# Attention scores of four heads on sixteen 32x32 tiles of TensorE instead of four strips of 32x128

## The chip, the cores and the metric

The kernel runs on one core of a Trainium2 chip. The metric is the device time of one execution in microseconds (us); the median of three runs is given, and beside it one execution that the hardware profiler recorded. TensorE (PE in the profile, its weight loads PEld) multiplies, VectorE (DVE) and ScalarE (ACT) work elementwise, GpSimd is POOL, SyncE is SP. SBUF is the working memory, and PSUM the memory that TensorE writes its results to.

## The reference, cut to what matters

Four layers are added to an image x of shape (2, 128, 64, 64) one after the other, each on a group-normalized x. Layer 1 is made of convolutions, layer 2 of a Fourier transform with products in the frequency domain, layer 3 is an attention with eight heads. The change is in layer 0, whose first attention has 4 heads of 32 channels over 64 x 64 = 4096 tokens:

```python
q1, k1, v, q2, k2 = jnp.split(qkv, 5, axis=1)
...
attn1 = jax.nn.softmax(jnp.einsum('bhnc,bhmc->bhnm', q1, k1) * temperature, axis=-1)
out1 = jnp.einsum('bhnm,bhmc->bhnc', attn1, v)
attn2 = jax.nn.softmax(jnp.einsum('bhnc,bhnd->bhcd', q2, k2) * temperature, axis=-1)
out2 = jnp.einsum('bhnc,bhcd->bhnd', v, attn2)
out = out1 + out2
```

Queries and keys are normalized beforehand. All of it is float32.

## The kernel before, in words

`tile_conv_preact_kernel` keeps x in SBUF and runs the four layers one after the other. A second, general version follows behind a flag and isn't executed with this input.

In layer 0 (`_layer0`, L1155) the 128 channels are the partitions: head j has partitions 32j to 32j+31 of `q1` and `k1`, each 128 x 4096. For each of the two batches the kernel first makes queries, keys and the first values, and then runs the attention `_attn_four` (L1084). That function goes over 8 blocks of 512 queries (`qb`) and, inside, 32 tiles of 128 keys (`kt`), 512 iterations over both batches. One iteration does the following.

- It takes two tiles `ps_s` of PSUM, each with two banks of 512 float32 per partition: the first for heads 0 and 1, the second for heads 2 and 3. The pool behind them, `spp`, has three such tiles (`bufs=3`), so the second tile of an iteration is the one that held the first pair's scores an iteration earlier. It can be written when the exponential of that pair has read it.
- Four matmuls (L1092), one for each head j, write the scores. The stationary operand is 32 channels x 128 keys of `k1`, the moving operand 32 channels x 512 queries of `q1`. Rows 32j to 32j+31 of the array are used with all 128 columns: a strip. The result is 128 keys x 512 queries, on all partitions of one bank; each head has its own bank.
- Two exponentials on ACT (L1102), each over one `ps_s` tile (128 x 1024), write the `weights` tiles in SBUF. `f0_p`, their pool, has six of them.
- `multiply` of the iteration *before* is called (a list `waiting` keeps it back by one). In it `four` (L1440) has four matmuls with a stationary operand of 128 keys x 32 channels of `vt` and a moving operand of 128 keys x 512 queries of the weights: all rows of the array, 32 columns for each head. They add into the accumulator `accs[0]`.
- For the softmax's sums, DVE adds the weights of four iterations (`sums`, L1459 and L1461, two instructions in each of three iterations out of four), and once in four iterations `four` multiplies the result with ones into `accs[1]`.

After 32 key tiles the accumulator is divided by the sums (L1469 to L1473).

A float32 matmul is two passes in TensorE's program, first and second pass side by side, each a weight load (LDWEIGHTS) and a MATMUL. So the four score matmuls are 8 loads and 8 MATMUL records in the profile, and so are the four value matmuls.

The order of work on each engine is the order in which the code issues it. The waits between engines are made by the tile framework from the tiles that are read and written: the first score matmul into a `ps_s` tile carries the wait for that tile, and the exponential waits for the last matmul of its pair. After every iteration `_layer0` (L1521) lets a generator `side` go one step further, two in the first 32 iterations: the remaining `values`, the channel attention of the second branch, and the normalization of the next batch. These steps put matmuls, transposes, DVE and ACT work between the iterations, until they are used up; then iterations follow on one another with nothing between them. `_attn_four` is called in layer 0 alone; layer 3 has an attention of its own (L1679, L1698).

Of the kernel before, what the change touches and what calls it, by code (L numbers as in the profile page):

```python
# [18 lines left out]
CH = 512  # L19
# [1064 lines left out]
def _attn_four(nc, p_pool, ps_pool, q, k, multiply):  # L1084

    waiting = []
    for qb in range(NCH):
        for kt in range(NQT):
            ps = [ps_pool.tile([128, 2, CH], F32, tag="sp", name="ps_s") for _ in range(2)]
            for j in range(4):  # L1090
                rows = slice(32 * j, 32 * j + 32)
                nc.tensor.matmul(  # L1092
                    ps[j // 2][:, j % 2, :],
                    k[rows, kt * 128 : (kt + 1) * 128],
                    q[rows, qb * CH : (qb + 1) * CH],
                    start=True,
                    stop=True,
                )
            w = []
            for p in range(2):  # L1100
                w.append(p_pool.tile([128, 2, CH], F32, tag="weights", name="weights"))
                nc.scalar.activation(w[p], ps[p], AF.Exp)  # L1102
            waiting.append((qb, kt, w))
            if len(waiting) > 1:
                multiply(*waiting.pop(0))
            yield
    for x in waiting:
        multiply(*x)
    yield
# [45 lines left out]
def _layer0(ctx, tc, X, a, cst, eps5, worst):  # L1155
# [354 lines left out]
    for b in range(B):  # L1510
        ss = small.tile([128, 4, 2 * len(BLOCKS)], F32, tag="ss", name="ss")
        w2 = small.tile([128, 128], F32, tag="w2", name="w2", bufs=1)
        ready[0] = 0
        run(queries_keys(ss))
        scale_queries(ss)
        run(values((0, 1)))
        side = [values((2, 3, 4)), channel_attention(ss, w2)]
        if b + 1 < B:
            side.append(normalize(b + 1))
        side = chain(*side)  # L1520
        for n, _ in enumerate(_attn_four(nc, pp, spp, q1, k1, multiply)):  # L1521
            next(side, None)
            if n < 32:
                next(side, None)
        run(side)
        run(finish(b, w2))
# [345 lines left out]
```

## Time and profile before

| what | value |
|---|---|
| median of 3 runs | 4988.65 us (4988.64 to 4990.94) |
| the profiled execution | 4991.73 us |
| its span, first to last instruction | 4989.9 us |
| mean granted clock of TensorE | 0.914 of full speed |
| busy: PE / ACT / DVE | 4458.1 / 3153.4 / 2291.3 us |
| instructions: PE, and as many weight loads | 38084 |
| score matmuls L1092, first and last start | 173.6 and 1933.1 us |
| layer 3's attention, first and last start of L1679 | 2995.7 and 4970.4 us |

A line of the costliest groups reads: line, engine, operation, output<-inputs, partitions x elements, count, then busy time and mean duration in ns of one, then the idle time of the engine just before and what ended most of it. Busy time is the union of overlapping instructions: eight matmuls that run side by side for 1 us are 1 us. For TensorE the form "32\*128" names the rows and columns of the array that are used. The chain that ended last is followed back from the last instruction to whatever released it; its shares add up to the span. In the 40 slices each digit is a busy share in tenths, and a slice is 125 us.

### The profile page before, as it was taken

What the parts mean: (1) busy time and instruction counts of PE and PEld (TensorE: products, weight loads), DVE (VectorE), ACT (ScalarE), POOL (GpSimd) and SP (SyncE); (2) the same over time, 40 slices, a digit from 0 to 9 for tenths busy, and PEclk for the clock granted to TensorE, in tenths of its full rate; (3) what the DMA queues carried; (4) which work ended last, traced back from release to release, by engine and by line L of the source; (5) the groups of instructions that cost most, each with busy time, mean ns of one, the idle gap of its engine ahead of it and who ended that gap; (6) DMA issues with size and microseconds to landing.
All of it is one profiled execution on the core that took longest, in us unless ns stands there. A gap on an engine that the chain in (4) does not pass through costs nothing.

```text
span 4989.9 us, 87747 instructions
## 1 busy us (share of the span) xinstructions
PE 4458.1 (89%) x38084; PEld 1792.5 (36%) x38084; DVE 2291.3 (46%) x3050; ACT 3153.4 (63%) x3539; POOL 53.4 (1%) x102
## 2 busy tenths in 40 slices
PE   6678899996889997996676789999999999999998
PEld 3222222241222223445565673333333333333332
DVE  5777678767777877997111142310122013100010
ACT  2445468824556884201011118999999999999998
POOL 1000000000000001000000000000000000000000
PEclk9788899997889999998676659999999999999999
DMA  1000000000000000006887600000000000000000
GB/s 40 0 1 1 1 1 1 1 1 1 1 1 1 1 1 6 1 0 108 126 127 121 89 7 3 5 5 6 5 5 5 6 5 5 5 6 5 6 5 6
DMA packets 154494, 90.06 MB, mean 18 GB/s; under 512 B 24553, under 2 KB 148457, under 8 KB 154098
## 3 DMA queue, kind: packets, MB, share of 16 engines
q1 hardware_dynamic: 154098, 84.36, 10.4%
q8 instruction: 300, 4.92, 0.4%
q14 instruction: 96, 0.79, 0.1%
HBM read 75.94 MB, written 4.19 MB: 16 GB/s over the span
## 4 chain that ended last, share of the span: by engine, by line
PE 78%; DVE 14%; issue 5%; ACT 2%; POOL 1%; DMA 0%; SPq 0%; ACTq 0%; DVEq 0%; POOLq 0%
PE ps_acc L1698 21%; PE ps_s L1679 17%; PE ps_acc L1440 11%; PE ps_s L1092 10%; DVE qk L1253 3%; PE ps_freq L827 3%; PE ps_acc L1315 2%; DVE X L612 2%; DVE sums L1461 2%; PE ps_pe L794 2%; DVE v L1253 2%; PE ps_bank L771 1%; PE ps_po L946 1%; PE ps_sp L1227 1%; DVE sums L1459 1%
## 5 line engine op out<-in xcount | busy, mean ns | idle before, releaser
L1689 ACT ACTIVATE weights<-ps_s 128x1024 f32<-128x1024 f32 x2048 | 1887.0, 1098 | 82.6 <-PE ps_s L1679 76.5
L1102 ACT ACTIVATE weights<-ps_s 128x1024 f32<-128x1024 f32 x1024 | 994.1, 1021 | 332.8 <-PE ps_s L1092 319.9
L1698 PE MATMUL ps_acc<-weights,vt 128*32 128x512 f32 x8192 | 1095.2, 607 | 0.0
L1679 PE MATMUL ps_s<-q,k 32*128 32x512 f32 x8192 | 926.6, 445 | 4.1 <-ACT weights L1689 3.3
L1092 PE MATMUL ps_s<-q,k 32*128 32x512 f32 x4096 | 686.6, 668 | 100.8 <-ACT weights L1102 100.7
L1679 PEld LDWEIGHTS ps_s<-q,k 32*128 32x128 f32 x8192 | 471.1, 183 | 847.5 <-ACT weights L1689 764.6
L1461 DVE TENSOR_TENSOR sums<-sums,weights 128x1024 f32<-128x1024 f32 x512 | 604.2, 1219 | 90.8 <-ACT weights L1102 90.8
L1440 PE MATMUL ps_acc<-weights,vt 128*32 128x512 f32 x4096 | 593.4, 633 | 12.0 <-ACT weights L1102 8.0
L1720 DVE COPY u<-ps_acc 128x512 f32<-128x512 f32 x32 | 22.1, 691 | 1005.3 <-PE ps_acc L1698 1005.3
L1092 PEld LDWEIGHTS ps_s<-q,k 32*128 32x128 f32 x4096 | 214.3, 191 | 535.9 <-issue 286.5
L1459 DVE TENSOR_TENSOR sums<-weights 128x1024 f32<-128x1024 f32 x256 | 303.7, 1218 | 192.3 <-ACT weights L1102 192.3
L1698 PEld LDWEIGHTS ps_acc<-weights,vt 128*32 128x32 f32 x8192 | 163.8, 108 | 379.1 <-issue 366.8
L612 DVE SCALAR_TENSOR_TENSOR X<-g,w,X 128x512 f32<-128x512 f32 x400 | 266.8, 741 | 0.1
L1440 PEld LDWEIGHTS ps_acc<-weights,vt 128*32 128x32 f32 x4096 | 85.6, 110 | 431.3 <-issue 393.4
L827 PE MATMUL ps_freq<-e,w_i 128*32 128x16 f32 x4224 | 140.2, 221 | 76.3 <-issue 76.3
L827 PE MATMUL ps_freq<-e,w_r 128*32 128x16 f32 x4224 | 142.8, 221 | 64.9 <-issue 64.4
L1253 DVE SCALAR_TENSOR_TENSOR qk<-pad,wd,qk 128x896 f32<-128x896 f32 (+2 forms) x160 | 171.1, 1069 | 4.1
L1440 PE MATMUL ps_acc<-sums,ones 128*32 128x512 f32 x1024 | 162.7, 608 | 3.5 <-DVE sums L1461 3.4
L827 PEld LDWEIGHTS ps_freq<-e,w_i 128*32 128x32 f32 x4224 | 131.9, 159 | 80.9 <-issue 80.8
L827 PEld LDWEIGHTS ps_freq<-e,w_r 128*32 128x32 f32 x4224 | 133.2, 159 | 69.1 <-issue 68.3
L837 ACT COPY pz<-ps_freq 128x272 f32<-128x272 f32 x16 | 6.8, 425 | 217.0 <-PE ps_freq L827 217.0
L837 DVE COPY pz<-ps_freq 128x256 f32<-128x256 f32 x16 | 6.8, 425 | 279.8 <-PE ps_freq L827 203.0
(237 smaller groups left out, 3276.7 us busy)
## 6 DMA issues: line engine op xcount, KB each, us to landing
w_r<-in_L_conv_kr_w SPq DMA_DIRECT2D x15, 528.0 KB, 12.2
w_r<-in_L_conv_kr_x SPq DMA_DIRECT2D x15, 528.0 KB
w_r<-in_L_conv_kr_y SPq DMA_DIRECT2D x15, 528.0 KB, 12.1
w_r<-in_L_conv_kr_z SPq DMA_DIRECT2D x15, 528.0 KB, 11.9
w_i<-in_L_conv_ki_w SPq DMA_DIRECT2D x15, 528.0 KB, 5.6
w_i<-in_L_conv_ki_x SPq DMA_DIRECT2D x15, 528.0 KB, 7.9
w_i<-in_L_conv_ki_y SPq DMA_DIRECT2D x15, 528.0 KB, 10.1
w_i<-in_L_conv_ki_z SPq DMA_DIRECT2D x15, 528.0 KB, 12.1
```

The source lines that it names most:

```text
L612: nc.vector.scalar_tensor_tensor(xi, g[:, i : i + ROWS, j : j + W], w8[:, s : s + 1], xi, ALU.mult, ALU.add)
L794: nc.tensor.matmul(pe[:, j * 6 * FW : j * 6 * FW + n * 3 * FW], yt[:, (r + j) * 128 : (r + j + 1) * 128], fwd_w[:, : n * 3 * FW], start=Tr ...
L827: nc.tensor.matmul(out.rearrange("p (x c) -> p x c", c=2), ws[n][:, :, s * FW + fw], e[:, s, :, :, 1 - n : 3 - n, fw].rearrange("p r b e - ...
L1092: nc.tensor.matmul(ps[j // 2][:, j % 2, :], k[rows, kt * 128 : (kt + 1) * 128], q[rows, qb * CH : (qb + 1) * CH], start=True, stop=True,)
L1102: nc.scalar.activation(w[p], ps[p], AF.Exp)
L1253: nc.vector.scalar_tensor_tensor(out, win, wd[:, grp, t : t + 1], out, ALU.mult, ALU.add)
L1440: nc.tensor.matmul(accs[n][rows, :], lhs(rows), w[j // 2][:, j % 2, :], start=first, stop=last)
L1459: nc.vector.tensor_add(parts[p], held[p], w[p])
L1461: nc.vector.tensor_add(parts[p], parts[p], w[p])
L1679: nc.tensor.matmul(ps[j // 2][:, j % 2, :], k[rows, kt * 128 : (kt + 1) * 128], q[n][rows, qb * CH : (qb + 1) * CH], start=(n == 0), stop= ...
L1689: nc.scalar.activation(w[p], ps[p], AF.Exp)
L1698: nc.tensor.matmul(ac[0][32 * j : 32 * j + 32, :], vt[:, kt, j // 2, i : i + 2, :].rearrange("p a d -> p (a d)"), w[j // 2][:, i, :], star ...
```

## The change

Each head's score matmul is cut into four by its keys. Strip i of 32 keys becomes a stationary operand of 32 channels x 32 keys, and its result goes to partitions 32i to 32i+31 of the same bank as before: a 32x32 tile of the array for each of four heads j and four strips i. The loop over strips is the outer one, so that all four heads come in turn within a strip. Sixteen matmuls with the same moving operands as before (each head's 512 queries are now streamed to four tiles) fill the same two `ps_s` tiles; exponentials, value matmuls and everything else stay as they are.

```diff
-            for j in range(4):
-                rows = slice(32 * j, 32 * j + 32)
-                nc.tensor.matmul(
-                    ps[j // 2][:, j % 2, :],
-                    k[rows, kt * 128 : (kt + 1) * 128],
-                    q[rows, qb * CH : (qb + 1) * CH],
-                    start=True,
-                    stop=True,
-                )
+            for i in range(4):
+                for j in range(4):
+                    rows, keys = slice(32 * j, 32 * j + 32), slice(32 * i, 32 * i + 32)
+                    nc.tensor.matmul(
+                        ps[j // 2][keys, j % 2, :],
+                        k[rows, kt * 128 + 32 * i : kt * 128 + 32 * i + 32],
+                        q[rows, qb * CH : (qb + 1) * CH],
+                        start=True,
+                        stop=True,
+                    )
```

## The prediction

> **What bounds the kernel now.** I read the page's slices first, then the chain that ended last, the costliest groups, the busy time of two stretches, the timeline of a few microseconds, and at last the starts of single instructions in it.
>
> ```profile
> PE   6678899996889997996676789999999999999998
> DVE  5777678767777877997111142310122013100010
> ACT  2445468824556884201011118999999999999998
> PEclk9788899997889999998676659999999999999999
> ...
> PE ps_acc L1698 21%; PE ps_s L1679 17%; PE ps_acc L1440 11%; PE ps_s L1092 10%; DVE qk L1253 3%; PE ps_freq L827 3%; PE ps_acc L1315 2%; DVE X L612 2%; DVE sums L1461 2%; PE ps_pe L794 2%; DVE v L1253 2%; PE ps_bank L771 1%; PE ps_po L946 1%; PE ps_sp L1227 1%; DVE sums L1459 1%
> ...
> L1102 ACT ACTIVATE weights<-ps_s 128x1024 f32<-128x1024 f32 x1024 | 994.1, 1021 | 332.8 <-PE ps_s L1092 319.9
> ...
> L1092 PE MATMUL ps_s<-q,k 32*128 32x512 f32 x4096 | 686.6, 668 | 100.8 <-ACT weights L1102 100.7
> ...
> L1440 PE MATMUL ps_acc<-weights,vt 128*32 128x512 f32 x4096 | 593.4, 633 | 12.0 <-ACT weights L1102 8.0
> ...
> L1092 PEld LDWEIGHTS ps_s<-q,k 32*128 32x128 f32 x4096 | 214.3, 191 | 535.9 <-issue 286.5
> ```
>
> One slice is 125 us. Layer 0's attention lies in 174 to 1938 us, and the changed matmuls (L1092) alone hold 10% of the chain. There are 2 batches x 8 query blocks x 32 key tiles = 512 iterations; 4096 records for 2048 score matmuls say that a float32 matmul is two passes, each with its own weight load.
>
> ```profile
> 800.00:900.00 100.00, 100.00 (x756) 26.19 (x752) 78.61 (x68) 80.62 (x84) 0.00 (x0) 1.00 0.00 1
> ...
> 400.00:500.00 100.00, 84.68 (x527) 25.07 (x530) 70.20 (x64) 58.69 (x64) 0.31 (x2) 0.87 0.00 1
> ```
>
> The columns after the length are PE, PEld, DVE, ACT, POOL, granted clock, DMA share and GB/s. In the first stretch there is no side work: TensorE never rests, at full clock. The same stretch holds 336 score records at eight an iteration, so 42 iterations in 100 us, **2.38 us each**. In the second, side work alternates with the attention and DVE shares the chain.
>
> ```profile
> 763.52 1.31 PE L1092 MATMUL ps_s<-q,k 32*128 32x512 f32 x8
> 764.76 1.94 ACT L1102 ACTIVATE weights<-ps_s 128x1024 f32<-128x1024 f32 x2 [0.18 <-PE ps_s L1092]
> 764.76 1.06 PE L1440 MATMUL ps_acc<-weights,vt 128*32 128x512 f32 x8
> 765.76 1.20 PE L1092 MATMUL ps_s<-q,k 32*128 32x512 f32 x8
> 766.89 1.06 PE L1440 MATMUL ps_acc<-weights,vt 128*32 128x512 f32 x8
> ```
>
> ```profile
> 779.93 1.00 PE ps_acc L1440 x8
> 780.92 1.07 PE ps_s L1092 x8
> 781.99 1.00 PE ps_acc L1440 x8
> 782.99 1.24 PE ps_s L1092 x8
> 784.23 1.54 PE ps_acc L1440 x8
> ```
>
> The second fence is the chain: the score group takes 1.07 and 1.24 us in turn, the value group 1.00. Every fourth iteration has a second group of ones, about 0.86 us more. The single starts show why 1.07 and 1.24 alternate. Three score tiles are in PSUM and an iteration takes two, so the second pair (heads 2, 3) waits for the exponential of the *first* pair of the iteration before. In a 1.24 group, heads 2 and 3 start some 180 ns after heads 0 and 1; in a 1.07 group, 13 ns or so after when that exponential is already done.
>
> **The numbers of one iteration**, from those starts at full clock:
> - weight load plus matmul of the next tile follow 6.7 ns after those of the tile before, though each matmul's second pass lies between them in program order: the second pass waits on its own tile and holds up no other.
> - first pass to second pass on one tile: 533 ns with 32x128 weights, 453 with 128x32 weights. Less 427 of streaming (512 columns; the value group's 8 records in two rounds show it), 106 and 26 remain: the first load, which nothing hides.
> - last second pass to the first instruction of the next group in another shape: 518 to 521 ns.
> - second pass of head 1 to the start of its exponential: 695 ns. Start of an exponential to the release of the score tile: 1075. Two exponentials start 920 apart.
>
> **What the Trainium skill says.** "TensorE: Matmul & The Clock Gate", section LDWEIGHTS, has a load take columns / 1.2 ns: 107 ns for 128 and 27 for 32; the 106 and 26 above agree. The same page, Part 3, gives 10.6x for sixteen 32x32 tiles with N=512, some 4 ns per tile, outputs in a bank for each row group: the arrangement of this change. No 32x32 matmul is in the trace of before; its 6.7 ns a tile in row and in column tiling is the nearest row. That part also says that matmuls keep program order; the trace differs, as second passes start after first passes of later tiles. "TensorEngine Tiling (Array Packing)", Key Properties, says that a change of mode drains the array; the 518 to 521 ns, some 92 over the streaming, agree, and both changes of mode remain.
>
> **The change part by part.**
> 1. *Passes on the array.* Four matmuls with 32x128 weights become sixteen with 32x32: 32 matmuls and 32 loads per iteration, for 8 and 8. If sixteen tiles run as independently as four rows or four columns do, each streams two passes as before. No gain or loss in streaming.
> 2. *Shorter first load*: 533 to 453, so 80 ns less per score group.
> 3. *Longer dispatch*: the last tile starts 15 x 6.7 = 100 ns after the first, for 20. Group length without a wait: 100 + 453 + 518 = 1.071, for 20 + 533 + 518 = 1.071. Points 2 and 3 cancel. The step's unknown size in 32x32 mode is bounded by about 1.7 ns (the offset between a load and its matmul here) and by 30 (four instructions at the 7.5 ns each that the layer 2 products at L827 sustain, 134 starts in 1 us). I take 6.7.
> 4. *The order of the wait.* The loop over key strips is outside that over heads. Head 2 of strip 0 is the third matmul of sixteen, and it is the one that waits for the score tile. Behind it on TensorE's queue stand thirteen others, among them strips 1 to 3 of heads 0 and 1. So the first pair is finished only after the wait; ACT's next exponential and then the value group wait for that. Before, heads 0 and 1 went ahead of it.
>
> The loop through this wait: third matmul to fourteenth (strip 3, head 1) 11 x 6.7 = 74; its second pass 453; exponential starts 695; release 1075: **2.297 us from one wait to the next**. TensorE alone needs 1.071 + 0.994 (value group) = 2.065. So each plain iteration that follows another waits 0.231 us. Before, the loop was 6 + 533 + 695 + 1075 = 2.309 from the *start* of the group, and a held second pair didn't delay the first, so the iteration after a held one had no wait: 2.296, 2.065, 3.156 (with ones), 2.065, sum 9.58 for four. (Measured: 4 x 2.38 = 9.52, so the recurrence is 0.6% long.) After: 2.300, 2.300, 3.160, 2.070, sum 9.83. The change makes three waits in four iterations of what were two: 0.25 / 4 = **0.062 us per iteration**.
>
> 5. *Where it counts.* The starts of the score groups give 286 iterations in the two plain stretches (700 to 1010 and 1560 to 1950 us), 225 in the others. Of these, DVE's side work ends many waits, and by the chain TensorE's attention lines, ACT's exponential and PE's other groups hold roughly 0.6 of the stretch; the rest hides it. 286 + 0.6 x 225 = 421 iterations x 0.062 = **26 us**. If nothing were hidden it is 32, if all of it in the mixed stretches 18.
> 6. *Added instructions* in PE's stream, 512 x 48 = 24,576 matmuls and loads: at zero, on the assumption that TensorE reads them in during the 1 us value group; without that cover, see the second rival. ACT, DVE, DMA and all other layers are untouched.
>
> The profiled execution has 4989.9 us of span and 1.8 around it, 4991.7 in all, 3 over the median of 4988.65. 4991.7 + 26 = 5017.8 for such a one, 4988.65 + 26 = **5015** for the median.
>
> **The rivals.**
> - *Not slower.* The shorter load wins: if the step per tile is below about 1.8 ns, as the 1.7 between load and matmul would allow, then the loop is 2.223 + 11 x 1.7 = 2.242 and the group 80 - 26 = some 50 ns shorter, and the recurrence falls to the 2.395 of before or just under. Price: down to -0.02 us x 421 = -9, so 4980 to 4990. For it: loads are a quarter as long. Against: 6.7 ns in both tilings. Chance 0.15 (0.05 of it below by over 0.2%).
> - *The sequencer can't keep up*: steps of 10 to 30 ns. Both the loop (11 steps) and the group (15) grow; 12 ns of average per ns of step, so at 20 ns 0.22 us x 421 = 92 us, 5080; at 30 ns 5130. For it: 64 instructions where 16 were, in bursts longer than any that the trace shows at 1.7 ns. Against: TensorE has a microsecond before each burst. Chance 0.17.
> - *Sixteen tiles aren't sixteen queues.* The trace never holds more than four second passes back at once. If only about eight can be, the tiles run in two waves, 0.45 us more in the loop and the group: 0.5 x 460 = 230 us, 5220. If tiles of one row group take turns, 3 x 0.88 us more for every iteration: 2.7 x 512, about 6370. For it: no such row in the trace. Against: one tile's second pass stops neither other rows in row tiling nor other columns in column tiling, which one queue per row or per column would not allow, and the 10.6x. Chance 0.13.
>
> **How the numbers follow.** The forecast (steps of 5 to 10 ns: 38 to 98 ns an iteration, 5005 to 5030) has 0.55. The range, 4984 to 5090, takes in the forecast, most of the sequencer's case and the upper part of the first rival; above it are the third rival and a few hundredths of the second, below it the best of the first, together 0.2. Runs of this kernel lie within 2.3 us, so 0.2% (10 us) is about what can be told from no change. Faster 0.05, same 0.10, slower 0.85.
>
> **What would show it.** Plain stretches at 2.44 to 2.47 us an iteration; score matmuls of shape 32x32 with 453 ns between their passes and 100 ns from the first to the last tile; heads 2 of strip 0 held in three of four iterations; later layers as long as before. An unheld group well over 1.1 us would show steps 3 or 1 wrong, an exponential that starts before the wait ends step 4.

## The result and the profile after

| | median | runs | profiled span |
|---|---|---|---|
| before | 4988.65 us | 4984.43 to 4990.94 (4) | 4989.9 us |
| after | 5013.7 us | 5008.7 to 5014.12 (4) | 5006.9 us |

The change makes the kernel slower: ratio 1.0049, 95% interval 1.0031 to 1.0066. The forecast was 5015 us. The sum came out; two of its terms did not, and they made up for each other. That is most of what follows.

The page of the changed kernel: slices, chain by line, and the groups that answer to those of before.

```profile
PE   6678899996889998897777789999999999999998
PEclk9889999997999999998666659999999999999999
...
PE ps_acc L1699 20%; PE ps_s L1680 17%; PE ps_acc L1441 11%; PE ps_s L1093 11%; DVE qk L1254 3%; PE ps_freq L827 3%; PE ps_acc L1316 2%; DVE X L612 2%; PE ps_pe L794 2%; DVE sums L1462 2%; DVE v L1254 2%; PE ps_bank L771 1%; PE ps_po L946 1%; PE ps_sp L1228 1%; PE ps_t L593 1%
...
L1103 ACT ACTIVATE weights<-ps_s 128x1024 f32<-128x1024 f32 x1024 | 994.1, 1021 | 353.5 <-PE ps_s L1093 341.4
...
L1093 PE MATMUL ps_s<-q,k 32*32 32x512 f32 x16384 | 738.4, 620 | 92.9 <-ACT weights L1103 91.9
...
L1093 PEld LDWEIGHTS ps_s<-q,k 32*32 32x32 f32 x16384 | 171.7, 104 | 586.3 <-PE ps_s L1093 247.4
```

Four times as many score matmuls keep TensorE busy for 738.4 us instead of 686.6, so the sixteen tiles do run side by side. The exponential's work is the same 994.1 us; its wait for the scores has grown from 319.9 to 341.4.

The chain in a plain stretch. First more of the kernel before than the prediction shows, then the changed kernel:

```profile
790.94 1.07 PE ps_s L1092 x8
792.01 1.00 PE ps_acc L1440 x8
793.00 1.24 PE ps_s L1092 x8
794.25 1.00 PE ps_acc L1440 x8
795.24 1.13 PE ps_s L1092 x8
796.37 1.00 PE ps_acc L1440 x8
797.37 1.18 PE ps_s L1092 x8
```

```profile
781.18 1.35 PE ps_s L1093 x32
782.53 1.00 PE ps_acc L1441 x8
783.53 1.34 PE ps_s L1093 x32
784.87 1.85 PE ps_acc L1441 x16
786.72 1.09 PE ps_s L1093 x32
787.81 1.00 PE ps_acc L1441 x8
788.81 1.36 PE ps_s L1093 x32
```

In what follows a score group is *held* when one of its matmuls waits for an exponential of the iteration before, and *free* when none does. Before, groups of 1.07 us are free. Those of 1.24, 1.13 and 1.18 are held, so over most of a query block three of four are, and not every other one as the prediction had it. After the change three groups of 1.34 us or more come for one of 1.09; the free one follows the value group that has a group of ones behind it (1.85 together). What ended the weight loads' idle time says the same. First the loads at L1092 of before, then those at L1093 of after, in us and times:

```profile
  ACT weights L1102: 241.9, 67
```

```profile
  ACT weights L1103: 257.8, 217
```

Waits for the exponential are three times as many.

Beyond what the page prints, I used the starts of single instructions in the traces: the length of each score group (first weight load to the first value matmul), the start of each iteration's first exponential, and the time at half of TensorE's clock. Iterations are counted from 0; 128 to 255 and 384 to 511 are plain; 0 to 128 and 256 to 352, the mixed stretches, have side work between them, apart from a plain part at their ends.

| | before | after |
|---|---|---|
| plain, us an iteration (both stretches) | 2.400 | 2.527 |
| mean score group there | 1.158 | 1.301 |
| groups over 1.21 us | 0.31 | 0.75 |
| iterations 0 to 128, us | 521.8 | 513.0 |
| iterations 256 to 352, us | 383.4 | 375.3 |
| half clock in those two, us | 138 and 96 | 83 and 61 |

So the plain stretches lose 16 us each, and the mixed ones *win* 17 together. Between the batches (iteration 255 to 256) 3 us more are lost.

### The profile page after: what moved, and what is told of

Read it like the earlier page. It is cut to its first block, busy times and chain, and to the rows that moved or that the text cites. A ratio compares the mean times of both kernels' runs of the same rounds, so it can differ in the third digit from the quotient of the medians.

```text
span 5006.9 us, 112346 instructions
## 1 busy us (share of the span) xinstructions
PE 4499.1 (90%) x50372; PEld 1749.0 (35%) x50372; DVE 2302.0 (46%) x3050; ACT 3153.5 (63%) x3539; POOL 55.7 (1%) x102
## 4 chain that ended last, share of the span: by engine, by line
PE 79%; DVE 14%; issue 5%; ACT 1%; POOL 1%; DMA 0%; SPq 0%; DVEq 0%; ACTq 0%; POOLq 0%
PE ps_acc L1699 20%; PE ps_s L1680 17%; PE ps_acc L1441 11%; PE ps_s L1093 11%; DVE qk L1254 3%; PE ps_freq L827 3%; PE ps_acc L1316 2%; DVE X L612 2%; PE ps_pe L794 2%; DVE sums L1462 2%; DVE v L1254 2%; PE ps_bank L771 1%; PE ps_po L946 1%; PE ps_sp L1228 1%; PE ps_t L593 1%
## 5 line engine op out<-in xcount | busy, mean ns | idle before, releaser
L1103 ACT ACTIVATE weights<-ps_s 128x1024 f32<-128x1024 f32 x1024 | 994.1, 1021 | 353.5 <-PE ps_s L1093 341.4
L1680 PE MATMUL ps_s<-q,k 32*128 32x512 f32 x8192 | 926.3, 444 | 4.1 <-ACT weights L1690 3.3
L1093 PE MATMUL ps_s<-q,k 32*32 32x512 f32 x16384 | 738.4, 620 | 92.9 <-ACT weights L1103 91.9
L1680 PEld LDWEIGHTS ps_s<-q,k 32*128 32x128 f32 x8192 | 470.5, 182 | 847.7 <-ACT weights L1690 764.8
L1093 PEld LDWEIGHTS ps_s<-q,k 32*32 32x32 f32 x16384 | 171.7, 104 | 586.3 <-PE ps_s L1093 247.4
```

The costliest lines, as they stand in the source:

```text
L1093: nc.tensor.matmul(ps[j // 2][keys, j % 2, :], k[rows, kt * 128 + 32 * i : kt * 128 + 32 * i + 32], q[rows, qb * CH : (qb + 1) * CH], star ...
L1680: nc.tensor.matmul(ps[j // 2][:, j % 2, :], k[rows, kt * 128 : (kt + 1) * 128], q[n][rows, qb * CH : (qb + 1) * CH], start=(n == 0), stop= ...
```

## The experiments

Two theories were put against each other for the plain stretches. **Wait order**: sixteen tiles cost nothing themselves, and the loss comes from heads 0 and 1 standing behind the wait of head 2. **Tile cost**: the sixteen tiles or their 64 instructions cost by themselves.

### Heads outside

```diff
-            for i in range(4):
-                for j in range(4):
+            for j in range(4):
+                for i in range(4):
```

> The sixteen 32x32 tiles as in the change, but the loop over heads outside and the loop over key strips inside, so that the wait for the second score tile stands at the ninth matmul and heads 0 and 1 are issued ahead of it. Wait-order theory (the cost comes from heads 0 and 1 standing behind the wait): score group without a wait 1.09 us as after the change, mean group in the plain stretches back at 1.14 to 1.17 us (after 1.30, before 1.16), 4983 to 4993 us. Tile-cost theory (sixteen tiles and 32 loads in place of 8 cost by themselves): the mean group stays at 1.25 to 1.30 us and the time at 5005 to 5015 us.

Measured: 4988.65 us against 4985.85 of the kernel before, ratio 1.0004 (0.9996 to 1.0013); plain stretches 2.395 us an iteration, mean group 1.149. Its chain:

```profile
776.86 1.09 PE ps_s L1093 x32
777.95 0.99 PE ps_acc L1441 x8
778.94 1.21 PE ps_s L1093 x32
```

The same sixteen tiles, with the wait at the ninth instead of the third, take as long as the four strips. With heads 0 and 1 ahead of the wait the tiles cost nothing; the change's loss needs its order.

### The four strips of before, with head 2 first

```diff
-            for j in range(4):
+            for j in (2, 0, 1, 3):
```

> The four 32x128 strips of the kernel before, but in the order of heads 2, 0, 1, 3, so that the matmul that waits for the second score tile comes first and heads 0 and 1 stand behind it. No 32x32 tile is in it. Wait-order theory: three of four groups are held, the mean group in the plain stretches is 1.25 to 1.32 us, 5005 to 5020 us. Tile-cost theory: nothing changes against the kernel before, 1.16 us a group, 4985 to 4992 us.

One thing is other than expected. In this program the tile framework gives the buffer that is still being read to the pair that is written second. So head 2 goes first without a wait, and it is head 0's matmul, second in the order, that waits for the exponential of the iteration before. In the trace a typical held group starts 884 ns after the start of that exponential, its second matmul 1075 ns after it. For the question it is the same: heads 0 and 1 can't finish before the wait ends.

Measured: 5000.36 us, ratio 1.0028 (1.0019 to 1.0038); plain 2.454 us, mean group 1.220, 0.72 of the groups over 1.21.

```profile
776.98 1.26 PE ps_s L1092 x8
778.25 1.00 PE ps_acc L1440 x8
779.24 1.26 PE ps_s L1092 x8
780.50 0.99 PE ps_acc L1440 x8
781.49 1.25 PE ps_s L1092 x8
782.75 1.32 PE ps_acc L1440 x8
784.07 1.07 PE ps_s L1092 x8
```

Three groups of 1.25 us or more and one free one appear without a single 32x32 tile, so a first pair that has to wait is enough for the pattern of the change. The time is under the 5005 expected, though, and the group is 0.062 us longer than before where the change has 0.143: wait order alone is less than half of it. The rest comes with the tiles, and mostly in held groups.

### Both kernels once more

> The kernel before once more, for a second profile. If the time that the mixed stretches gave back after the change (iterations 0 to 128 and 256 to 352, some 17 us in the two profiles) is chance of one execution, this profile's mixed stretches differ from those of the first by as much, and the time at TensorE's half clock in them lies anywhere between 140 and 230 us. If it belongs to the change, they repeat to within 4 us and the half clock stays at 200 to 240 us.

> The changed kernel once more, for a second profile. If the give-back belongs to the change, iteration 128 starts again 5 to 10 us earlier than in the kernel before, and the half clock in the mixed stretches is again 130 to 160 us; the plain stretches have 0.14 us more an iteration. If it is chance, the mixed stretches take as long as before or longer and the span is 5012 us or more.

The programs are unchanged. One run each: 4986.52 and 5010.22 us. The mixed stretches repeated: 522.3 and 383.4 us before, 513.5 and 375.3 after, half clock 138 and 96 against 87 and 61. The 17 us belong to these programs and aren't chance of one execution. What comes behind layer 0's attention can vary more: 3048.5 us from its last exponential to the end in this run of before, 3055.3 in the first (3053.8 and 3053.7 after). That explains most of why the two first profiles lie 17 us apart and the medians 25.

### The attention with no side work in it

```diff
-        run(values((0, 1)))
-        side = [values((2, 3, 4)), channel_attention(ss, w2)]
+        run(values((0, 1, 2, 3, 4)))
+        run(channel_attention(ss, w2))
         if b + 1 < B:
-            side.append(normalize(b + 1))
-        side = chain(*side)
-        for n, _ in enumerate(_attn_four(nc, pp, spp, q1, k1, multiply)):
-            next(side, None)
-            if n < 32:
-                next(side, None)
-        run(side)
+            run(normalize(b + 1))
+        run(_attn_four(nc, pp, spp, q1, k1, multiply))
```

> The kernel before with layer 0's side work (remaining values, channel attention, next normalization) run ahead of the attention instead of between its iterations, so that all 512 iterations follow on one another. Slower in all than the kernel before, by a few hundred us, since the side work is no longer hidden. Both theories: groups alternate as in the plain stretches, 2.36 to 2.42 us an iteration, mean score group 1.16 us. It is the base for the next run.

> The changed kernel with the side work ahead of the attention in the same way. If the cost of an iteration is that of the plain stretches of the two profiles, 0.143 us, it takes 512 x 0.143 = 73 us (65 to 80) more than the run without interleaved side work of the kernel before, 2.9% of nothing hidden. If it is the 0.062 us of the prediction, 32 us (25 to 40).

Measured: 5043.65 and 5109.28 us (ratios to the kernel before 1.0118, 1.0101 to 1.0135, and 1.0245, 1.0228 to 1.0262). The difference is 66 us, 0.128 us for each of 512 iterations, and the plain stretches show 2.400 and 2.527 again. The 73 expected were too many, since a group's length isn't an iteration's. Early in each query block one of the fourth iteration's exponentials waits for VectorE's sums. In the kernel before, at 700 to 1000 us, that is (us in total, times, longest):

```profile
ACT weights L1102 <- DVE sums L1459: 2.4, 4, 0.6
```

Some of the change's delay falls into that wait. The fifth score group of a block is 0.28 us longer after the change, but from its start to the next group's it takes 2.57 us for 2.78. That 0.49 us, spread over 32 iterations, is nearly all of the 0.016 between 0.143 and 0.127. The expectation of the first run missed as well: taking the side work out of the attention cost the kernel before 57 us, not a few hundred.

The page of the second, whose score groups are never cut by other work:

```profile
L1093 PE MATMUL ps_s<-q,k 32*32 32x512 f32 x16384 | 709.5, 604 | 0.4 <-ACT weights L1103 0.4
```

So the change costs 66 us when no side work is between the iterations, against 25 in the kernel as it stands. Most of the difference lies in iterations 0 to 128 and 256 to 352, where the change gains 17 us there and loses 24 here.

### Another placing of the side work

```diff
-            if n < 32:
+            if n < 64:
                 next(side, None)
```

> The kernel before with two steps of side work in each of the first 64 iterations instead of the first 32, so that the side work meets other iterations. Some 4970 to 5010 us. It is the base for the next run: other alignment, same work.

> The changed kernel with the same other placing of the side work. If the mixed stretches give back time because of the change itself, they are 5 to 10 us shorter again than in the run of the kernel before with this placing, with less half clock, and the two runs differ by 20 to 30 us. If the give-back depends on how side work and iterations happen to meet, the mixed stretches differ by another amount or the other sign and the two runs are 30 to 65 us apart; the plain stretches show 0.127 us an iteration either way.

Measured: with four strips 4957.27 us (0.9938, 0.9923 to 0.9953), with sixteen tiles 5010.44 (1.0046, 1.0031 to 1.0062): 53 us apart, not 25. The other placing alone makes the kernel before 29 us faster, more than its expectation allowed. The mixed stretches now *lose* with the change: 514.0 against 503.1 us for iterations 0 to 128, 385.1 against 382.2 for 256 to 352, with half clock 90 and 84 us against 114 and 86. So the 17 us are no property of the change alone: they turn with the placing of the side work. What in the placing does it isn't shown. Less half clock doesn't go with less time here, so it isn't shown to be the cause.

### What else a held group pays: how many tiles stand before the signal

Call the time from the start of the first pair's last second pass to the start of its exponential the signal. In the trace of before it is 634 ns in three of four groups of the plain stretches and 694 in most of the others; eight of 254 are longer, behind the wait for VectorE. The changed kernel has 725 or 726 ns in half of its groups, from the fourteenth tile, and 754 (the free groups) or 786 in most of the others. (The expectations below say 722 for the 725.) The next runs vary the number of tiles before the first pair's last pass. Two strips of 64 keys, strips outside:

```diff
-            for i in range(4):
+            for i in range(2):
                 for j in range(4):
-                    rows, keys = slice(32 * j, 32 * j + 32), slice(32 * i, 32 * i + 32)
+                    rows, keys = slice(32 * j, 32 * j + 32), slice(64 * i, 64 * i + 64)
...
-                        k[rows, kt * 128 + 32 * i : kt * 128 + 32 * i + 32],
+                        k[rows, kt * 128 + 64 * i : kt * 128 + 64 * i + 64],
```

> Eight 32x64 tiles: two strips of 64 keys, strips outside and heads inside, so that the wait is still at the third matmul with heads 0 and 1 of the second strip behind it. Signal theory (the exponential starts later after its pair's last second pass the more tiles stand before that pass, 630 ns with two to four tiles, 722 with fourteen, so some 7 ns a tile): 650 to 680 ns here, a held group of 1.22 to 1.28 us, mean group 1.18 to 1.24 us, 4990 to 5003 us. If the longer signal belongs to column tiles as such: 720 ns or more, mean group about 1.25 us or more, 5003 us or more.

Measured: 4980.24 us, 0.9985 (0.9979 to 0.9992); 654 ns in half of the groups, 675 and 714 in the others; held groups mostly 1.237 to 1.298, mean 1.221, plain 2.449 us. The signal is where expected, and the time is 10 us under: the plain stretches lose 6 us each against before, and the mixed ones win 20 (509.1 and 376.1 us). By the previous pair of runs such a gain can turn with the placing, so it isn't shown to be a merit of the tiles.

Sixteen tiles, with head 2's first tile ahead, then the eight tiles of heads 0 and 1, then the rest:

```diff
-            for i in range(4):
-                for j in range(4):
+            order = [(0, 2)] + [(i, j) for i in range(4) for j in (0, 1)]
+            order += [(i, j) for i in range(4) for j in (2, 3) if (i, j) != (0, 2)]
+            for i, j in order:
+                if True:
```

> The sixteen 32x32 tiles with the waiting matmul (head 2, strip 0) first, then the eight of heads 0 and 1, then the other seven of heads 2 and 3. The whole group is still held by the wait, as after the change, but the first pair ends with the ninth tile in place of the fourteenth. Signal theory (some 7 ns more for each tile ahead): the exponential starts 670 to 700 ns after the pair's last second pass (after the change 722 or more), the loop is about 5 x 7 + 40 = 75 ns shorter, mean group 1.22 to 1.26 us (after 1.30), 4998 to 5008 us. If the 722 ns belongs to 32x32 tiles whatever their number: 722 ns again and 1.27 to 1.29 us, since only the 35 ns of dispatch go.

Measured: 4998.28 us, 1.0021 (1.0014 to 1.0029); 690 ns in half of the groups, 704 and 750 in the others; mean group 1.237, plain 2.469.

```profile
776.56 1.28 PE ps_s L1095 x32
777.85 1.00 PE ps_acc L1443 x8
778.84 1.27 PE ps_s L1095 x32
```

Here, too, it is head 0's first tile, the second in the order, that waits. Of the 0.143 us that the change adds to a group, this order leaves 0.079.

Where the first pair ends behind the wait, a loop of four parts sets the length of a held group: from the wait to the first pass of the pair's last tile, from there to its second pass, the signal, and 1077 ns from the start of the exponential to the end of the next wait. Less 994 ns for the value group this is the group's length:

| kernel | the four parts, ns | sum less 994 | held group, ns |
|---|---|---|---|
| 32x32, the change | 82 + 453 + 726 + 1077 | 1344 | 1343 |
| strips, head 2 first | 7 + 533 + 634 + 1077 | 1257 | 1256 |
| 32x64, strips outside | 20 + 480 + 654 + 1077 | 1237 | 1236 |
| 32x32, head 2, then first pair | 50 + 453 + 690 + 1077 | 1276 | 1276 |

The last column is the held group behind an iteration with the frequent signal; a signal 60 ns longer makes the next group 60 ns longer (1404 ns after the change). So between the change and the strips with head 2 first, 75 ns are dispatch, 92 are signal, and 80 come off for the shorter load.

The most frequent signal in the plain stretches, by the number of score tiles up to and with the one whose pass ends the pair:

| kernel | tiles before the signal | signal, ns |
|---|---|---|
| before; strips, head 2 first | 2; 3 | 634; 634 |
| 32x64, heads outside; strips outside | 4; 6 | 654; 654 |
| 32x32, heads outside; head 2, then first pair | 8; 9 | 694; 690 |
| 32x32, the change | 14 | 726 |

From the first row to the last it rises by 92 ns, on average some 8 ns a tile. Within one shape, though, two or three tiles and four or six give the same, and only from eight or nine to fourteen does it rise, by 32 to 36 ns; the rest comes from one shape to the next. "TensorE: Matmul & The Clock Gate", Part 3, in its section on the per-tile semaphore tail, gives 4.7 ns a tile for the tail behind a packed group, besides what each increment costs. The direction agrees, the table's average is larger, and the equal values within a shape don't fit a price per tile. What makes the signal late isn't shown: shape and number change together in this table.

### A version that is faster than both

Two strips of 64 keys as above, with the loops exchanged so that heads are outside, and the wait is at the fifth tile.

> The same eight 32x64 tiles with heads outside, so that the wait is at the fifth matmul and heads 0 and 1 are ahead of it. First load of 64 columns 53 ns instead of 107, eight tiles 47 ns from first to last: a group without a wait takes 1.04 to 1.05 us (before 1.07). The loop through the exponential is 20 + 480 + 640 + 1075 = 2.215 us from the group's start (before 2.25). Wait-order theory: mean group 1.10 to 1.14 us (before 1.16), and 4965 to 4985 us, faster than both kernels. If the time stays at 4983 to 4993 us, the group's length is given back in other waits.

Measured: 4963.56 us, 0.9956 (0.9943 to 0.997); plain 2.376 us, mean group 1.128. The time is a little under the range expected. The gain on the kernel before is small, 23 us, but a ratio of 1 lies outside its interval. In this piece of the chain the free group is 1.04 and the held one 1.21:

```profile
778.18 1.04 PE ps_s L1093 x16
779.22 1.00 PE ps_acc L1441 x8
780.22 1.21 PE ps_s L1093 x16
```

With the other placing of the side work as well:

> Eight 32x64 tiles with heads outside, and two steps of side work in each of the first 64 iterations. If both gains add (23 us of the first, 29 us of the second), 4930 to 4940 us. If the gain of the placing depends on how side work and iterations meet, as the runs of the changed kernel with that placing say, anything from 4925 to 4970 us, with the plain stretches at 2.375 us an iteration.

Measured: 4954.53 us, 0.993 (0.9917 to 0.9944). The two gains don't add: it is 3 us under four strips with that placing, and the two intervals overlap. Only the 3 us in each plain stretch (301.7 against 304.9) are sure to be the tiles'.

## Why the prediction was right, step by step

1. *Passes* (step 1): right. In the trace the second passes of all sixteen start 453 ns after their first passes, and up to sixteen are held back at once. The free group is 1.089 us with sixteen tiles, 1.073 with four. The rival of too few queues is out.
2. *First load and dispatch* (steps 2 and 3): the load is right, 453 ns instead of 533. The dispatch is nearly right: steps of 6.7 ns, but the last two tiles come 15 and 17 ns apart, so that it is 120 ns from the first load to the last first pass where 100 were predicted. The two points therefore don't quite cancel, which is the 16 ns of the free group. After a wait the eleven steps from the third tile to the fourteenth take 82 ns, for 74 predicted. The sequencer's rival is out too.
3. *The order of the wait* (step 4): right in mechanism, as the first two experiments show from both sides, and for after in number (0.75 of the groups are held). Its size was off: a mean group is 0.143 us longer and an iteration 0.127, for 0.062. The term that failed is the 695 ns from the pair's last pass to its exponential, taken for both kernels from one group. Before it is mostly 634, and the waits, put at 0.231 us in two of four groups, lengthen three by some 0.17, 0.06 and 0.11: 0.34 in four iterations, not 0.46. After it is 725 to 786, and the held groups, put at about 0.235 over a free one in three of four, are 0.25 to 0.32 over it: 0.84, not 0.70. The 2.38 us of an iteration, against which the sum of before was tried, was read off 42 of them; over the whole plain stretches it is 2.400.
4. *Where it counts* (step 5): wrong. The plain stretches lost 0.127 x 254 = 32 us where 18 were expected (0.062 for 286), and the mixed ones gave 17 back where 8 more were expected lost. The share of the chain that TensorE holds in a stretch was read as a fraction of cost that counts. It says nothing of what a later start of one group does where side work stands between, and that had either sign: minus 17 us with one placing, plus 14 with another. Why stays open.
5. *Added instructions* (step 6): at nothing, nearly right. A free group would show them, and it is longer by the 16 ns of point 2 alone.

The forecast of 26 us is thus close because a loss that was put at about half its size and a gain that wasn't foreseen made up for each other. The direction was earned, the closeness was luck.

## What to carry to other kernels

Before a group of matmuls is cut finer, look at which of them waits and what stands behind it: work for the next engine's earliest start goes ahead of the wait, and reordering loops can be worth more than the shape of the tiles. Check afterwards which tile waits: where buffers go round, a new order can move the wait to another tile, as it did twice here. Take each term of a loop through two engines from many groups, not from one, since in a loop a term of 60 ns comes back every iteration. Where a stretch is shared with side work, measure the change with the side work elsewhere as well: the gain or loss there can be the placing's.

## What the runs showed of the hardware that was not expected

- In each of these kernels two of the common signals lie 60 ns apart: 634 and 694 before, 694 and 754 with 32x32 tiles and heads outside, 654 and 714 with both kernels of two strips, 726 and 786 after the change. Where the wait is ahead of the first pair's last tile, a third value lies between them (754 after the change, 675 with two strips and strips outside). What sets the 60 ns isn't shown.
- The value group (128x32) starts 517 to 518 ns after the last second pass of the scores in nearly every plain iteration of all these kernels, whether the score tiles are 32x128, 32x64 or 32x32: this time doesn't depend on the number of tiles.
- Two executions of the same program agree within 0.5 us in each stretch of the attention, half-clock time included to within 4 us, while what comes behind it moved by 7 us in one pair of executions and by 0.1 in the other.
